# New ranks for the row of maxima and for the two parts of queries and keys in a planned attention stack

## The chip, the cores and the metric

The kernel runs on one core of a Trainium2 chip. The metric is the device time of one execution in microseconds, as a median over runs. A profiled execution gives the trace from which all other times here are read.

## The reference

The input is 16 sequences `x` of 256 tokens with 256 features, and 16 contexts of 120 tokens with 256 features. Four blocks follow each other; all attention has 16 heads of 16 features:

- `l0` and `l1`: cross attention on the context, then `layernorm(attention(x) @ Wo + bo + x)`.
- the third block: causal self attention on 256 tokens (`ms`), cross attention (`cs`) and a feed-forward of 256 to 1024 to 256 features (`ff`), each on a layer norm of `x` and added to `x`.
- `l3`: cross attention with weights rounded to -1, 0 and 1 times a scale, added to `x`.

```python
q = split_heads(x @ Wq.T + bq); k = split_heads(ctx @ Wk.T + bk); v = split_heads(ctx @ Wv.T + bv)
probs = softmax(einsum("bqhd,bkhd->bhqk", q, k) / 4 (+ mask))
x = einsum("bhqk,bkhd->bqhd", probs, v).reshape(B, S, D) @ Wo.T + bo (+ x, layer norm)
```

## The kernel before

Sequences are worked on in pairs: 8 pairs by 6 layers. The pairs of the layers are interleaved by the offsets `OFF`, so that at any time two or three layers are in work.

**Parts.** To keep float32 accuracy from the fast matmul format, a number is held as a high part, rounded to that format, and a low part, the remainder. `split2` makes both for queries and keys out of the projection in PSUM: the high part on ACT (line L784) or on DVE (L785), then the low part on DVE (L787), into a tile `h_q_…` or `h_k_…`. There are three such tiles for all layers. From them SP issues DMAs that stack the parts of each head in rows of `qst` (three issues for a query tile, L826 twice and L829) and `kst` (six issues for keys, L848).

**Maxima.** A first pass of scores (L918 in cross attention, L971 in self attention) goes to PSUM, two banks at a time. DVE reduces them to negated maxima in a tile `neg` (L903, 352 instructions). `put_max` then transposes `neg` on PE (L890, 80 times), copies 32 rows of it out of PSUM as `negt` on ACT or DVE (L423 or L424), and SP writes it as two rows into `qst` (L892). The second pass of scores (L936, L993) multiplies with these rows too, and so has the maximum already subtracted; ACT takes the exponential of it (L907), and PE multiplies with the values (L949, L1009, L1010). The result is transposed on DVE (L855, L871), divided, split and projected (L770); POOL adds it to `x` (L695). L770 is also where the projections of queries, keys and values are.

**The order.** No engine's order is written by hand. `Sched` records every operation with the engines that it may run on, a cost on each, and what it reads and writes. There are 6,364 of them. `run` then plays them through with those costs. An operation joins an engine's queue when the plan has all its inputs ready; when the engine comes free, the one with the lowest key that also finds its buffers goes next. The key is the operation's number in the order of recording, minus what it is put ahead, plus what it is put behind. The order found so is the order of the instructions on each engine; on the chip each engine executes its list in that order and waits on semaphores. SP's DMA issues are ranked in the same way. A running instruction or group of matmuls is not interrupted.

The ranks that stand beside the changed ones: the second pass of scores is 200 ahead (`ST_AHEAD`), the reductions 100 behind (`MAX_BEHIND`), the output projection and the matmuls with the values of a cross attention 200 behind, the mask rows on SP 200 ahead, loads of `x` on SP 50 ahead, the steps of layer norm 50 ahead. `put_max` and `split2` have no rank of their own.

```python
o.key = o.idx - self.ahead                # in op()
heapq.heappush(queue[e], (o.key, o.idx, o))   # in assign()
o.key += MAX_BEHIND                       # in max_op()
```

Of the kernel before, what the change touches and what calls it, by code (L numbers as in the profile page):

```python
# [11 lines left out]
F32 = mybir.dt.float32  # L12
# [8 lines left out]
P = 128  # L21
# [35 lines left out]
X_AHEAD = 50  # L57
SPLIT_AHEAD = 100
SELF_BEHIND = 200
MAGIC = 1.5 * 2.0**23  # L60


# [13 lines left out]
MAX_ROW = MASK_ROW + 1  # L76
# [48 lines left out]
class Sched:  # L125
# [64 lines left out]
    def op(self, alts, r=(), w=(), acq=(), nbytes=0, port=False):  # L190

        o = Op()
        o.alts, o.nbytes, o.port, o.idx = alts, nbytes, port, len(self.ops)
        o.key = o.idx - self.ahead
        deps, uses = set(), []
        for k in (*r, *w, *acq):
            h = k[0] if isinstance(k, tuple) else k
            if h not in uses:
                uses.append(h)
        for k in r:  # L200
            h, sub = k if isinstance(k, tuple) else (k, None)
            hit = False
            for s2, (wr, rd) in h.keys.items():
                if sub is None or s2 is None or s2 == sub:
                    deps.update(wr)
                    rd.append(o)
                    hit = True
            if not hit:
                h.keys[sub] = ([], [o])
        for k in w:  # L210
            h, sub = k if isinstance(k, tuple) else (k, None)
            for s2, (wr, rd) in h.keys.items():
                if sub is None or s2 is None or s2 == sub:
                    deps.update(wr)
                    deps.update(rd)
            if sub is None:
                h.keys.clear()
            h.keys[sub] = ([o], [])
        deps.discard(o)
        o.deps, o.uses = deps, uses  # L220
        for h in uses:
            h.uses += 1
        self.ops.append(o)
        return o
# [119 lines left out]
def cross_stack_kernel(ctx: ExitStack, tc, x, xT, ctxT, mask, w, w1, w2, cols, b1, rows, out):  # L344
    nc = tc.nc
    NP = xT.shape[0] // 2
    ACT, DVE, POOL, PE, SP = nc.scalar, nc.vector, nc.gpsimd, nc.tensor, nc.sync
# [5 lines left out]
    sc = Sched()  # L353
# [14 lines left out]
    def sb(tag, shape, dt, nm, kind=None):  # L368
        return sc.handle(tag, lambda i: work.tile(shape, dt, tag=f"{tag}{i}", name=nm, bufs=1), kind)
# [3 lines left out]
    def bank(nm, kind=None):  # L373
        return sc.handle("ps", lambda i: banks[:, i, :], kind)
# [11 lines left out]
    def pe(cost, fn, r=(), w=(), acq=(), cls="r", ahead=0):  # L386

        o = op({"PE": (cost, fn)}, r, w, acq)
        o.cls = cls
        o.key -= ahead  # L390
        return o
# [8 lines left out]
    def dve(n, fn, r=(), w=(), acq=(), port=False):  # L400
        return op({"DVE": (T_DVE(n), fn)}, r, w, acq, port=port)
# [4 lines left out]
    def dma(fn, nbytes, r=(), w=(), n=1, acq=(), each=420.0, ahead=0):  # L406

        o = op({"SP": (each * n, fn)}, r, w, acq, nbytes)
        o.count = n
        o.key -= ahead  # L410
        return o
# [8 lines left out]
    def cast(n, out, a, r, w, psum_src=False, acq=()):  # L420

        return op({
            "ACT": (T_ACT(n) + (0 if psum_src else 34), lambda: ACT.copy(out(), a())),  # L423
            "DVE": (T_DVE(n if psum_src else n / 2), lambda: DVE.tensor_copy(out(), a())),  # L424
        }, r, w, acq, port=not psum_src)
# [12 lines left out]
    ident = const.tile([P, P], F32, tag="ident", name="ident")  # L438
# [25 lines left out]
    flat = lambda t: t.rearrange("p a b -> p (a b)")  # L464
# [129 lines left out]
    def quant(t, nm):  # L594
# [10 lines left out]
        dve(256, lambda: DVE.tensor_scalar(t(), t(), 2.0, -2.0, ALU.min, ALU.max), r=[t], w=[t], port=True)  # L605
        dve(256, lambda: DVE.tensor_scalar(t(), t(), MAGIC, MAGIC, ALU.add, ALU.subtract), r=[t], w=[t], port=True)
        dve(256, lambda: DVE.tensor_scalar(t(), t(), 1.0, -1.0, ALU.min, ALU.max), r=[t], w=[t], port=True)
# [172 lines left out]

    def split2(ps, src, bias, hi, lo, h2, key, n, r):

        op({
            "ACT": (T_ACT(n, 1), lambda: ACT.activation(hi(), src(), AF.Identity, bias=bias())),  # L784
            "DVE": (T_DVE(n), lambda: DVE.tensor_scalar(hi(), src(), bias(), None, ALU.add)),  # L785
        }, [ps, *r], [(h2, (key, 0))])
        dve(n + 62, lambda: DVE.scalar_tensor_tensor(lo(), src(), bias(), hi().bitcast(F32), ALU.add, ALU.subtract), r=[ps, *r, (h2, (key, 0))], w=[(h2, (key, 1))])  # L787

    def project_heads(W, x_of, bias, high, n, nm, r):

        h2 = sb("h2", [P, 2, 2, S], F32R, f"h2_{nm}")
        ps = bank(f"pj_{nm}")
        br, bcol = ([bias], lambda f: bias()[:, f : f + 1]) if isinstance(bias, Handle) else ([cols_in], lambda f: bias[:, f : f + 1])

        def half_(f):
            o = ps if later.keys else later
            pe(2 * len(terms(W)) * f1(n), lambda: mm_wx(ps()[:, f * S : f * S + n], W, lambda m: m[:, f * P : (f + 1) * P], x_of),
               r=[*W, *r], w=[(ps, f)] if later.keys else [(ps, f), later], acq=[h2])

        def parts(f):  # L800
            split2(ps, lambda: ps()[:, f * S : f * S + n], lambda: bcol(f), lambda: h2()[:, f, high, :n], lambda: h2()[:, f, 1 - high, :n], h2, f, n, br)

        half_(0)
        half_(1)
        parts(0)
        parts(1)

        return h2
# [78 lines left out]
    def put_max(neg, q, nm):  # L887
        ps = bank(f"negp_{nm}")
        negt = sb("negt", [32, P], F32R, f"negt_{nm}")
        pe(110, lambda: PE.transpose(ps()[:, :P], neg(), ident), r=[neg], w=[ps], acq=[negt])  # L890
        cast(128, negt, lambda: ps()[:32, :P], [ps], [negt], psum_src=True)
        dma(lambda: SP.dma_start(flat(q().bitcast(F32))[MAX_ROW : MAX_ROW + 2], negt().bitcast(F32)), 16384, r=[negt], w=[(q, "max")], each=720.0)  # L892

    def new_max():
        neg, made = new_neg()
# [13 lines left out]
    def attend_cross(q, k, b, v, wo, p, nm, x_, dst):  # L909
# [13 lines left out]
        for t in range(2):  # L923
            for j0 in (0, 4):
                s1(t, j0)
        put_max(neg, q, nm)
        t1 = [sb("t1", [P, 2, 8, 32], F32, f"t1_{nm}_{c}") for c in range(2)]

# [28 lines left out]
    def attend_self(q, k, v, wo, p, b, nm, x_):  # L957
# [18 lines left out]
        for t in range(2):  # L976
            for j0 in range(0, 8, 4 >> t):
                s1(t, j0)
        put_max(neg, q, nm)
        t1 = [sb("t1", [P, 2, 8, 32], F32, f"t1_{nm}_{c}") for c in range(2)]  # L980

# [21 lines left out]
        def values(pv, c, pr0, pr1):  # L1003
# [7 lines left out]

            pe(1370, mm, r=[*pr0, pr1, *v], w=[pv], cls="p", ahead=-SELF_BEHIND)

# [326 lines left out]
```

## Time and profile before

| what | value |
|---|---|
| median of 3 runs | 1227.35 us (1226.05 to 1229.39) |
| profiled execution: its own time, its span | 1234.49 us, 1232.8 us |
| busy share of PE, weight loads, DVE, ACT, POOL | 95%, 85%, 78%, 65%, 60% |
| granted TensorE clock, mean | 0.979 of full speed |

PE is TensorE's matmuls and PEld its weight loads, which overlap them; DVE is VectorE, ACT ScalarE, POOL GpSimd, and SP the engine that issues DMAs. A name followed by q (SPq) is the engine's sequencer. In a list of waits a line gives the engine and the work that waited, what it waited for, the sum in us, the number of waits and the longest. In a timeline a line gives start, duration, engine, line, operation, output and inputs, and how many instructions stand in it. The chain of waits is followed back from the last instruction of the execution to what released each one.

### The profile page before, as it was taken

The numbers are of one execution on the slowest core, as the hardware profiler recorded it, in microseconds if no ns is written. First come the engines' busy times: TensorE is split into PE (matmuls) and PEld (weight loads), VectorE is DVE, ScalarE is ACT, GpSimd is POOL, SyncE is SP. The second block draws the span as 40 slices with busy tenths as digits, with TensorE's granted clock in tenths as the row PEclk, the third lists the DMA queues.
The fourth block names the chain that finished last, engine by engine and source line by source line (L and its number), as shares of the span: only waits on it lengthen the run. The fifth ranks groups of instructions, "written<-read, shape, count | busy, mean of one in ns | idle before, by whom it ended". The sixth has DMA issues, their size and how long they took to land.

```text
span 1232.8 us, 29450 instructions
## 1 busy us (share of the span) xinstructions
PE 1169.1 (95%) x10972; PEld 1052.3 (85%) x10972; DVE 958.9 (78%) x1809; ACT 798.1 (65%) x1356; POOL 743.7 (60%) x1011
## 2 busy tenths in 40 slices
PE   6898999999998899999999999998999999999996
PEld 5887788888887788898988888887999999999864
DVE  7687678988886887787798899999634666767886
ACT  4566676667676575677665566677576667766754
POOL 3268566666777797889865556566533236445432
PEclk9799999999998999999999999998999999999989
DMA  8698688666754835544455766772321344435651
GB/s 219 170 257 220 172 243 212 184 179 180 187 142 114 210 101 139 141 131 117 129 148 143 201 169 178 189 197 80 128 76 60 96 112 118 136 91 162 146 129 45
DMA packets 155095, 186.42 MB, mean 151 GB/s; under 512 B 13806, under 2 KB 119624, under 8 KB 154952
## 3 DMA queue, kind: packets, MB, share of 16 engines
q1 hardware_dynamic: 154952, 184.54, 55.7%
q8 instruction: 87, 1.43, 0.5%
q14 instruction: 56, 0.46, 0.1%
HBM read 54.22 MB, written 29.39 MB: 68 GB/s over the span
## 4 chain that ended last, share of the span: by engine, by line
PE 63%; DVE 10%; DMA 8%; POOL 7%; ACT 7%; issue 5%; SPq 1%; POOLq 0%; ACTq 0%; DVEq 0%
PE banks L770 25%; PE banks L918 7%; PE banks L1123 6%; PE banks L936 6%; PE banks L949 6%; DVE neg L903 3%; PE banks L993 3%; PE banks L971 3%; PE banks L737 2%; DMA qst<-h_q_l 2%; PE banks L1009 2%; ACT pr_l L907 1%; POOL pr_ms L1000 1%; DMA qst<-negt_l 1%; DVE t_l L855 1%
## 5 line engine op out<-in xcount | busy, mean ns | idle before, releaser
L903 DVE TENSOR_REDUCE neg<-banks 128x8 f32<-128x960 f32 (+1 forms) x352 | 400.5, 1162 | 53.5 <-PE banks L918 29.8
L907 ACT ACTIVATE pr_l<-banks 120x1024 f32<-120x1024 f32 x192 | 190.0, 1028 | 39.5 <-PE banks L936 37.5
L918 PE MATMUL banks<-kst,qst 97*128 97x240 f32 x1024 | 160.5, 290 | 9.0 <-DMA qst<-h_q_l 2.9
L936 PE MATMUL banks<-qst,kst 99*120 99x256 f32 x1024 | 158.8, 290 | 10.3 <-DMA qst<-negt_l 4.1
L918 PEld LDWEIGHTS banks<-kst,qst 97*128 97x128 f32 x1024 | 136.9, 197 | 24.0 <-issue 10.8
L936 PEld LDWEIGHTS banks<-qst,kst 99*120 99x120 f32 x1024 | 134.9, 186 | 21.7 <-DVE neg L903 7.3
L423 ACT COPY oc<-banks 128x512 f32<-128x512 f32 x94 | 55.1, 587 | 86.0 <-PE banks L770 67.3
L907 ACT ACTIVATE pr_ms<-banks 128x1024 f32<-128x1024 f32 x96 | 95.3, 1032 | 18.4 <-PE banks L993 17.9
L1123 PE MATMUL banks<-w,h1hl_ff 128*128 128x256 f32 x768 | 104.0, 284 | 1.4 <-DVE h1hl_ff L1117 1.3
L770 PE MATMUL banks<-thl_ff,w 128*128 128x256 f32 x768 | 102.2, 283 | 0.1
L695 POOL TENSOR_TENSOR x_l<-oc,x_l 128x512 f32<-128x512 f32 x48 | 62.2, 1295 | 63.6 <-ACT oc L423 63.6
L1123 PEld LDWEIGHTS banks<-w,h1hl_ff 128*128 128x128 f32 x768 | 96.2, 189 | 3.4 <-DVE h1hl_ff L1117 2.3
L949 PE MATMUL banks<-pr_l,vau 120*32 120x256 f32 x1536 | 96.4, 392 | 0.9 <-DVE negt_l L424 0.4
L770 PEld LDWEIGHTS banks<-thl_ff,w 128*128 128x128 f32 x768 | 95.4, 189 | 0.7 <-issue 0.4
L1117 DVE TENSOR_TENSOR h1hl_ff<-h_ff,h1hl_ff 128x512 fp32r<-128x512 f32 x64 | 48.2, 754 | 59.5 <-ACT h1hl_ff L423 56.5
L417 POOL TENSOR_TENSOR cc_l<-t_l,rec_l 128x256 f32<-128x256 f32 x87 | 55.5, 657 | 50.5 <-DVE rec_l L865 48.1
L1000 POOL TENSOR_SCALAR_AFFINE_SELECT pr_ms<-pr_ms 128x512 f32<-128x512 f32 (+1 forms) x96 | 75.4, 800 | 11.3 <-ACT pr_ms L907 11.0
L417 POOL TENSOR_TENSOR cthl_l<-ct_l,cthl_l 128x512 fp32r<-128x512 f32 x42 | 54.1, 1288 | 43.8 <-ACT cthl_l L423 40.1
L1113 ACT ACTIVATE h_ff<-banks,b1t 128x256 f32<-128x256 f32 x119 | 50.3, 472 | 46.5 <-PE banks L770 40.8
L949 PEld LDWEIGHTS banks<-pr_l,vau 120*32 120x32 f32 x1536 | 45.8, 112 | 34.4 <-issue 4.1
L907 ACT ACTIVATE pr_cs<-banks 120x1024 f32<-120x1024 f32 x64 | 64.2, 1029 | 14.6 <-PE banks L936 12.9
L993 PE MATMUL banks<-qst,kst 99*128 99x128 f32 (+1 forms) x512 | 71.2, 281 | 2.6 <-DMA qst<-negt_ms 1.6
(311 smaller groups left out, 2776.5 us busy)
## 6 DMA issues: line engine op xcount, KB each, us to landing
qst<-h_q_l SPq DMA_DIRECT2D x144, 256.0 KB
kst<-h_k_l SPq DMA_DIRECT2D x144, 120.0 KB
kst<-h_k_ms SPq DMA_DIRECT2D x96, 128.0 KB
qst<-h_q_ms SPq DMA_DIRECT2D x48, 256.0 KB
qst<-h_q_cs SPq DMA_DIRECT2D x48, 256.0 KB
xd<-x_l SPq DMA_DIRECT2D x32, 256.0 KB
x_l<-xd SPq DMA_DIRECT2D x32, 256.0 KB
chl_l<-chl SPq DMA_DIRECT2D x16, 512.0 KB
```

What stands on the lines that cost most here:

```text
L417: "POOL": (T_POOL(n, per), lambda: POOL.tensor_tensor(out(), a(), b(), alu)),
L423: "ACT": (T_ACT(n) + (0 if psum_src else 34), lambda: ACT.copy(out(), a())),
L695: pool(512, lambda: POOL.tensor_tensor(fl(), o(), fl(), ALU.add), r=[o, t], w=[t])
L770: PE.matmul(ps, lhs(i, c), rhs(j, c), start=(n == 0), stop=(n == 2 * len(pairs) - 1))
L903: o = dve(2 * n * keys, lambda: DVE.tensor_reduce(out(), src(), AX.X, ALU.max, negate=True), r=[ps, *made], w=[(neg, (t, j0))])
L907: act(1024, lambda: ACT.activation(pr()[:keys], st()[:keys], AF.Exp, scale=0.25), r=[st], w=[pr])
L918: PE.matmul(ps()[:, j // 2, (j % 2) * 2 * SK : (j % 2 + 1) * 2 * SK], q()[:MAX_ROW, j0 + j, t * P : (t + 1) * P], kk(j0 + j)[:MAX_ROW], st ...
L936: PE.matmul(st()[:SK, i, g * S : (g + 1) * S], kk(2 * u + i)[:ROWS, g], q()[:ROWS, 2 * u + i, :], start=True, stop=True)
L949: PE.matmul(pvs[c]()[32 * a : 32 * a + 32, h * S : (h + 1) * S], window(v[0](), c * 8 + a * 2 + h)[:SK], prs[2 * c + h]()[:SK, a // 2, (a ...
L993: PE.matmul(st()[:, i, o * n : (o + 1) * n], k()[:ROWS, j, g, kt * P : (kt + 1) * P], q()[:ROWS, j, kt * P :], start=True, stop=True)
L1000: pool(2 * per * P, lambda: POOL.affine_select(v_(), v_(), pattern=[[0, 2 * per], [1, P]], base=0, channel_multiplier=-1, compare_op=ALU.i ...
L1123: PE.matmul(yo[b]()[:, t * D : (t + 1) * D], hl()[:, i, c * S + t * P : c * S + (t + 1) * P], two(w2s[k // 2][j]())[:, c, :], start=(k == ...
```

## The change

Two operations of `put_max`, the transpose on PE and the DMA on SP, get a key that is 150 lower; the copy between them keeps its key. Both operations of `split2`, the high and the low part of queries and keys, get a key that is 75 higher. No operation is added or removed, and none changes its size.

```diff
+PUT_AHEAD = 150
+
+SPLIT_BEHIND = 75
@@ split2
+        sc.ahead = -SPLIT_BEHIND
         op({
             "ACT": (T_ACT(n, 1), lambda: ACT.activation(hi(), src(), AF.Identity, bias=bias())),
             "DVE": (T_DVE(n), lambda: DVE.tensor_scalar(hi(), src(), bias(), None, ALU.add)),
         }, [ps, *r], [(h2, (key, 0))])
         dve(n + 62, lambda: DVE.scalar_tensor_tensor(lo(), src(), bias(), hi().bitcast(F32), ALU.add, ALU.subtract), r=[ps, *r, (h2, (key, 0))], w=[(h2, (key, 1))])
+        sc.ahead = 0
@@ put_max
-        pe(110, lambda: PE.transpose(ps()[:, :P], neg(), ident), r=[neg], w=[ps], acq=[negt])
+        pe(110, lambda: PE.transpose(ps()[:, :P], neg(), ident), r=[neg], w=[ps], acq=[negt], ahead=PUT_AHEAD)
         cast(128, negt, lambda: ps()[:32, :P], [ps], [negt], psum_src=True)
-        dma(lambda: SP.dma_start(...), 16384, r=[negt], w=[(q, "max")], each=720.0)
+        dma(lambda: SP.dma_start(...), 16384, r=[negt], w=[(q, "max")], each=720.0, ahead=PUT_AHEAD)
```

More of the change, by code (lines that the diff above doesn't have):

```diff
@@ L889, in put_max @@
         negt = sb("negt", [32, P], F32R, f"negt_{nm}")
-        pe(110, lambda: PE.transpose(ps()[:, :P], neg(), ident), r=[neg], w=[ps], acq=[negt])
+        pe(110, lambda: PE.transpose(ps()[:, :P], neg(), ident), r=[neg], w=[ps], acq=[negt], ahead=PUT_AHEAD)
         cast(128, negt, lambda: ps()[:32, :P], [ps], [negt], psum_src=True)
-        dma(lambda: SP.dma_start(flat(q().bitcast(F32))[MAX_ROW : MAX_ROW + 2], negt().bitcast(F32)), 16384, r=[negt], w=[(q, "max")], each=720.0)
+        dma(lambda: SP.dma_start(flat(q().bitcast(F32))[MAX_ROW : MAX_ROW + 2], negt().bitcast(F32)), 16384, r=[negt], w=[(q, "max")], each=720.0, ahead=PUT_AHEAD)
     def new_max():
```

## The prediction

> **What bounds the kernel now.** I began with the page's busy times, then read busy time in stages, then what PE waited for, then the chain of waits, and last two short timelines around a row of maxima.
>
> ```profile
> PE 1169.1 (95%) x10972; PEld 1052.3 (85%) x10972; DVE 958.9 (78%) x1809; ACT 798.1 (65%) x1356; POOL 743.7 (60%) x1011
> ```
>
> ```profile
> 30.00:200.00 170.00, 157.78 (x1447) 138.96 (x1450) 130.06 (x224) 104.59 (x172) 98.02 (x102) 0.95 0.79 210
> 1000.00:1233.00 233.00, 218.22 (x1994) 195.02 (x1992) 171.91 (x328) 153.36 (x275) 106.11 (x144) 0.97 0.45 120
> ```
>
> The last table's columns are the window, its length, busy time of PE, PEld, DVE, ACT and POOL, the granted clock, the DMA share and GB/s. PE is the bound nearly everywhere: 1232.8 - 1169.1 = 63.7 us without a matmul in flight, of which some 11 us fall into the first 30 us. The other gaps are spread: 12.2 us in the first window shown, where DMA is at 0.79, 14.8 us in the second, the rest between. No work is taken away by the change, so all it can win is a part of these gaps. What ended them (engine, work that waited, releaser: sum in us, times, longest):
>
> ```profile
> PE banks L890 <- DVE neg L903: 4.2, 6, 1.9
> PE banks L936 <- DMA qst<-negt_l: 4.1, 3, 2.7
> PE banks L918 <- DMA qst<-h_q_l: 2.9, 3, 1.8
> PE banks L918 <- DVE neg L903: 2.9, 6, 1.2
> ...
> PEld banks L936 <- DVE neg L903: 7.3, 8, 2.9
> PEld banks L918 <- DVE neg L903: 5.7, 11, 1.4
> ```
>
> The reductions (L903) are the most frequent partner: they hold PSUM banks in pairs and they feed the transpose. On PE they end 4.2 + 2.9 us here and 2.0 us in three smaller rows (L936 0.8, L971 0.7, L993 0.5), together 9.1 us; on the weight loads 7.3 + 5.7 us here, and 4.0, 1.7 and 1.1 us for L890, L971 and L993, 19.8 us. The maxima's DMA ends 4.1, 1.6 (negt_ms) and 1.5 us (negt_cs) on PE: 7.2 us. What the splits end themselves on PE (L787 behind L770, L936, L949, L737) is 0.8 + 0.6 + 0.5 + 0.4 + 0.3 = 2.6 us, and the stacks made of them 2.9 us (above) and 0.4 us (kst, before L971), 3.3 us. The chain says the same with other weights:
>
> ```profile
> PE 63%; DVE 10%; DMA 8%; POOL 7%; ACT 7%; issue 5%; SPq 1%; POOLq 0%; ACTq 0%; DVEq 0%
> PE banks L770 25%; PE banks L918 7%; PE banks L1123 6%; PE banks L936 6%; PE banks L949 6%; DVE neg L903 3%; PE banks L993 3%; PE banks L971 3%; PE banks L737 2%; DMA qst<-h_q_l 2%; PE banks L1009 2%; ACT pr_l L907 1%; POOL pr_ms L1000 1%; DMA qst<-negt_l 1%; DVE t_l L855 1%
> ```
>
> L903 has 3% of it, the stack of queries 2%, the row of maxima 1% in the `l` layers. Neither side of the trade is off the path.
>
> **How far a rank reaches.** 6,364 recorded operations over 1232.8 us are 5.2 ranks a microsecond; 150 ranks are 29 us of recording, 75 ranks 14.5 us. A rank decides only between operations that are ready together on one engine; it makes none ready.
>
> **The transpose on PE (80 of about 0.3 us).** Two timelines show what it waits for:
>
> ```profile
> 596.39 2.34 DVE L903 TENSOR_REDUCE neg<-banks 128x4 f32<-128x1024 f32 x2
> 598.27 1.65 PE L770 MATMUL banks<-ms_o,cthl_ms 128*128 128x256 f32 x12
> 599.25 2.58 SPq L848 DMA_DIRECT2D kst<-h_k_ms  x4
> 599.75 0.27 PE L890 MATMUL banks<-ident,neg 128*128 128x128 f32 x1
> 600.48 0.25 ACT L423 CAST negt_ms<-banks 32x128 fp32r<-32x128 f32 x1
> 601.88 0.66 SPq L892 DMA_DIRECT2D qst<-negt_ms  x1
> ...
> 622.75 1.84 PE L1234 MATMUL banks<-cols,w 128*128 128x1 f32 x16
> 624.46 0.31 PE L890 MATMUL banks<-ident,neg 128*128 128x128 f32 x1
> 625.08 0.70 SPq L892 DMA_DIRECT2D qst<-negt_ms  x1
> ```
>
> The last maximum ends at 596.39 + 2.34 = 598.73 and the transpose starts 1.02 us later, right behind a group of 12 matmuls that was already running; at 624.46 it again follows the group that ran when the maximum ended. The next matmuls, the query projection, come after it. A lower key cannot interrupt a group, and here no second group went ahead. I book 0, between a gain of the 4.2 us that PE waits ahead of L890 and, as a transpose chosen before other work can at most displace a group, a loss of its own 80 x 0.3 = 24 us if every one opened a gap (nothing shows one). What hides an earlier transpose is the projection that otherwise runs first; if none is ready, PE has nothing to lose.
>
> **The row on SP (80 issues of 0.69 us).** In the first timeline the copy ends at 600.73 and the issue starts at 601.88, 1.15 us late, because SP was issuing a key stack of four; in the second it is issued at once (624.80 + 0.26 = 625.06, then 625.08). A lower key can remove this lateness, not the flight that follows:
>
> ```profile
> 372.77 5.23 DMA qst<-negt_l
> 676.54 2.37 DMA qst<-negt_ms
> ```
>
> PE's 7.2 us of waits for rows are the most that can go. Seven waits, about half of them behind a late issue, and under 1 us regained in each of those (a half of the 1.15 us): 3.5 x 0.55 = 1.9, booked as -1.5, between 0 and -7.2 us. In return each row that overtakes sets a stack issue back by 0.69 us, and when its copy is late on the chip SP stands still with the stacks behind it; SP already stands 27.0 us for copies by ACT alone in the list of its waits. PE waits for stacks only 3.3 us, so I book +0.5, between 0 and +3.
>
> The Trainium skill's page "DMA: Bandwidth & Descriptors", section "Anatomy of one DMA", puts about 2.0 us of a DMA down to fixed cost, mostly the receipt of the write. By that figure (fitted on GpSimd's path, while SP issues here) most of the 2.37 us flight above would be out of a rank's reach, which speaks against this part; counted strictly, its -1.5 would be 0 and the sum below -3.5.
>
> **The splits behind (512 operations).** The low parts are 256 on DVE at about 0.47 us; of the high parts 185 are on ACT at 0.47 us and 71 on DVE at 0.48 us. No busy time changes. Until now a split went ahead of a reduction recorded up to 100 ranks before it (the reductions are 100 behind); now the lead is 25 ranks. So DVE will more often take a reduction of 1.16 us first, and a layer-norm step, the split following it by one such piece. Gain: a reduction one split (0.47 us) earlier frees two banks and brings the transpose nearer. The waits on L903 bracket it with 9.1 us by PE and 19.8 us by the weight loads; a load that waits delays PE only when nothing is in flight, so I take their middle, 14.5 us, and as a split of 0.47 us earlier is about 40% of a reduction's 1.16 us, I take 40%: -6. Ends: 0 and -13 (two thirds of 19.8).
>
> The page "Perfetto Trace Analysis", section "Identifying the Most-Contended Engine", holds matmul busy time for a bad measure of the room left and takes the share of weight loads. By it the 85% row, not the 95% row, is the one to read, and the term would be 40% of 19.8, that is -8 and a sum of -7; a mean of the two rows stays my value.
>
> Loss: behind a delayed split stand the SP issues of its stack (three for queries, six for keys) and whatever SP has behind them, one of the three h2 tiles, and the bank of the projection. The PE waits on splits and stacks are 2.6 + 3.3 = 5.9 us now. A third more is +2: most stacks land well ahead of the first pass of scores, which the other interleaved layer covers. If that cover is gone, each of these gets longer by a whole reduction. Ends: 0 and +10, see the second rival.
>
> **Sum.** 0 - 1.5 + 0.5 - 6 + 2 = -5 us. The profiled execution took 1234.49 us (span 1232.8 and 1.7 around it), which gives 1229.5 for it. It lies 7.1 us above the median of the runs, 1227.35, and above all three; a shift of the schedule moves both alike, so I predict 1222.4. About 0.3% (3.7 us) is what a measurement can tell from no change, so below 1223.7 counts as faster and above 1231.0 as slower. What is late next is the exponential on ACT (L907 waiting on L936, 37.5 us) and the DMA flights.
>
> **Rival 1: the ranks hardly do anything.** Ready operations rarely compete: ACT and DVE are idle 35% and 22% of the time, the two transposes waited for running groups only, and half of the rows were issued at once. Then the order changes in places, with small gains and losses: 1224 to 1231, say 1227. For it speaks the spread of small waits, against it that one exchange shifts the lists of all five engines after it. Chance 0.24.
>
> **Rival 2: the query stacks become the wait.** Place: the first 400 us, where DMA is at 0.79 and the chain goes through these transfers:
>
> ```profile
> 137.19 5.87 DMA qst<-h_q_l
> 157.22 3.59 DMA qst<-h_q_l
> 162.30 4.04 DMA qst<-h_q_l
> ```
>
> The chain gives them about 2%, some 21 us or five flights of 4 us. If each starts one reduction later, 5 x 1.16 = +5.8 us. A gap then also costs clock: after one in 404.00:408.00 (PE busy 0.59 of 4.00 us) the next 4 us were granted 0.57, or 1.7 us lost. With one such gap more, +7.5 us: 1235. It decides if at least half of the five flights follow a split that DVE now takes after a reduction and the gain on the reductions stays at 0. Against it: the projections of the next pairs cover them now. Chance 0.32.
>
> **How the numbers follow.** The forecast has 0.44, its own range 1213 to 1223.7 (the low end is the sum with -13 and -1.5 and the losses at 0). The whole range reaches to rival 2's price and a little over: 1213 to 1236. Chances: 0.44 faster, 0.24 same, 0.32 slower.
>
> **What would show it.** Right: waits of PE and PEld on DVE L903 fall from 9.1 and 19.8 us by a third; SP issues L892 within 0.1 us of its copy nearly always; busy times stay as they are; gaps fall from 63.7 to about 59 us. Wrong: the chain's DMA qst<-h_q_l above 2%, more waits of L918 and L971 on stacks, more slices with a lowered clock before 400 us. The forecast falls if the waits on L903 shrink and PE's gaps don't, since then another releaser took their place.

## Result and profile after

The changed kernel takes 1241.0 us (median of 4 runs, 1235.5 to 1246.4) where the kernel before, run beside it on the same chip, takes 1228.4 us. The ratio is 1.0084, 95% interval 1.0058 to 1.0111: slower by 12.6 us by the medians. The quotient of the two medians is 1.0103, a little more than the ratio on record; per cents of the change below are the ratio's. The profiled execution after took 1240.46 us with a span of 1238.7; that is only 6.0 us above the profiled execution before, which lay 6 us above its kernel's median. So the two profiles show about half of the loss, and small differences between them are read with care.

The page of the changed kernel, busy times, and then its chain of waits (shares by engine, then by line). Lines of `kernel.py` have moved: L770, L890, L892, L903, L918, L936 and L949 are now L774, L896, L898, L909, L924, L942 and L955.

```profile
PE 1166.6 (94%) x10972; PEld 1052.7 (85%) x10972; DVE 968.2 (78%) x1825; ACT 791.4 (64%) x1339; POOL 748.5 (60%) x1012
```

```profile
PE 59%; DVE 13%; POOL 8%; DMA 6%; ACT 6%; issue 6%; SPq 1%; POOLq 0%; DVEq 0%; ACTq 0%
PE banks L774 24%; PE banks L1129 7%; PE banks L924 7%; PE banks L942 6%; PE banks L955 6%; DVE neg L909 5%; PE banks L999 2%; PE banks L977 2%; PE banks L741 2%; ACT pr_l L913 2%; PE banks L1015 1%; DVE t_l L861 1%; DMA qst<-negt_l 1%; POOL pr_ms L1006 1%; DMA kst<-h_k_ms 1%
```

PE has 1238.7 - 1166.6 = 72.1 us without a matmul (63.7 before). The chain gives the reductions 5% instead of 3%, DVE 13% instead of 10%, and the stack of queries has gone from the list. What ended PE's gaps and the weight loads' (sum in us, times, longest):

```profile
PE banks L774 <- DVE cthl_l L428: 3.6, 2, 3.0
PE banks L924 <- DMA qst<-h_q_l: 3.4, 3, 1.6
PE banks L896 <- DVE neg L909: 3.3, 4, 1.3
PE banks L955 <- DVE neg L909: 3.2, 1, 3.2
PE banks L774 <- POOL cthl_l L421: 2.6, 4, 0.9
PE banks L924 <- DVE neg L909: 2.5, 6, 0.9
...
PE banks L977 <- DVE neg L909: 2.3, 4, 0.9
PE banks L942 <- DMA qst<-negt_l: 2.1, 4, 1.0
...
PEld banks L924 <- DVE neg L909: 7.7, 16, 1.2
```

Adding up all rows of a kind: reductions 9.1 us before, 13.0 after; the turned outputs of attention (`cthl`, high and low part, ahead of the output projection) 6.8 and 10.4; the rows of maxima 7.2 and 2.9; query stacks 2.9 and 3.4, key stacks 0.4 and 1.1. On the weight loads the reductions went from 20.2 us (the prediction's 19.8 leaves out two rows of 0.2) to 24.2 us.

One place shows what a new order can do. Two windows of the kernel before and after, with the prediction's columns (window, length, PE, PEld, DVE, ACT, POOL, granted clock, DMA share, GB/s); first before:

```profile
84.00:88.00 4.00, 4.00 (x36) 3.92 (x35) 2.09 (x6) 3.70 (x7) 2.54 (x2) 1.00 1.10 286
88.00:92.00 4.00, 4.00 (x51) 3.29 (x53) 3.57 (x4) 2.59 (x5) 3.21 (x3) 1.00 1.05 351
```

then after:

```profile
84.00:88.00 4.00, 1.21 (x6) 0.72 (x5) 1.44 (x3) 1.95 (x5) 2.14 (x3) 0.81 1.07 349
88.00:92.00 4.00, 4.00 (x20) 4.00 (x21) 0.00 (x0) 1.26 (x2) 1.69 (x2) 0.50 0.73 244
```

and the timeline of the changed kernel that leads to them (start, duration, engine, line, operation, idle before and its releaser):

```profile
70.13 1.94 ACT L913 ACTIVATE pr_l<-banks 120x1024 f32<-120x1024 f32 x2 [2.37 <-PE banks L942]
...
76.98 1.59 PE L774 MATMUL banks<-l_o,cthl_l 128*128 128x256 f32 x12
...
79.18 2.21 DVE L909 TENSOR_REDUCE neg<-banks 128x8 f32<-128x960 f32 x2
...
79.39 1.93 PE L955 MATMUL banks<-pr_l,vau 120*32 120x256 f32 x32
...
81.31 0.48 DVE L792 SCALAR_TENSOR_TENSOR h_q_l<-banks,cols,h_q_l 128x256 fp32r<-128x256 f32 x1
...
81.70 1.31 DVE L861 STREAM_TRANSPOSE t_l<-banks 128x512 f32<-128x512 f32 x2
...
86.37 0.53 PE L774 MATMUL banks<-l_o,cthl_l 128*128 128x256 f32 x1 [1.97 <-ACT cthl_l L427]
...
87.72 2.71 PE L774 MATMUL banks<-l_o,cthl_l 128*128 128x256 f32 x11 [0.81 <-POOL cthl_l L421]
```

The same attention in the kernel before:

```profile
76.19 1.03 ACT L907 ACTIVATE pr_l<-banks 120x1024 f32<-120x1024 f32 x1
...
76.79 1.93 PE L949 MATMUL banks<-pr_l,vau 120*32 120x256 f32 x32
...
79.37 1.30 DVE L855 STREAM_TRANSPOSE t_l<-banks 128x512 f32<-128x512 f32 x2
...
80.88 2.16 DVE L903 TENSOR_REDUCE neg<-banks 128x8 f32<-128x960 f32 x2
```

After, DVE takes two reductions and then a low part, and turns the output of this attention at 81.70; before, the same turn started at 79.37, ahead of the reductions at 80.88. That looks like DVE's doing, but the turn's input came late. Its matmuls with the values ended on PE at 78.72 before and at 81.32 after, and the turn followed them by 0.65 us before and by 0.38 us after. Nor did these matmuls lack their input: the last exponential that they need had ended at 72.07 after, against 77.22 before. PE's own new list put other groups ahead of them until 79.39, among them the output projection at 76.98. Everything behind the turn (reciprocal, division on POOL, second turn, high and low part) is a chain, and at 84.40 the next entry of PE's list is the projection of this output: PE stands 1.97 and 0.81 us. The plan has the same hole: in its play-through PE is without work for some 3 us ahead of this projection. Then the next 4 us were granted half the clock, and 11 matmuls took 2.71 us where 12 of the same kind took 1.59 at 76.98.

At the same share of all matmuls done, the changed kernel is 4.3 us behind the one before at 109 us, about 1 us behind at 354, about 1 us ahead at 600, and 5 to 6 us behind from 935 us on. So what this place cost was regained; no single place holds the loss, and the place shows how an exchange costs, not where the loss of the whole kernel arises.

The Trainium skill, page "TensorE: Matmul & The Clock Gate", Part 1, "What's actually happening", has the clock go back to half after an idle window of about 3.4 us. In narrower windows of this trace the granted clock was 1.00 up to 86.25 us, 0.50 from 86.50 to 93.25, and 1.00 again from 93.50. So it fell at the end of the first gap of 1.97 us, ahead of the second of 0.81: a single gap as long as the page's window was not needed here.

### The profile page after: what moved, and what is told of

Read it like the earlier page. It is cut to its first block, busy times and chain, and to the rows that moved or that the text cites. A ratio compares the mean times of both kernels' runs of the same rounds, so it can differ in the third digit from the quotient of the medians.

```text
span 1238.7 us, 29440 instructions
## 1 busy us (share of the span) xinstructions
PE 1166.6 (94%) x10972; PEld 1052.7 (85%) x10972; DVE 968.2 (78%) x1825; ACT 791.4 (64%) x1339; POOL 748.5 (60%) x1012
## 4 chain that ended last, share of the span: by engine, by line
PE 59%; DVE 13%; POOL 8%; DMA 6%; ACT 6%; issue 6%; SPq 1%; POOLq 0%; DVEq 0%; ACTq 0%
PE banks L774 24%; PE banks L1129 7%; PE banks L924 7%; PE banks L942 6%; PE banks L955 6%; DVE neg L909 5%; PE banks L999 2%; PE banks L977 2%; PE banks L741 2%; ACT pr_l L913 2%; PE banks L1015 1%; DVE t_l L861 1%; DMA qst<-negt_l 1%; POOL pr_ms L1006 1%; DMA kst<-h_k_ms 1%
## 5 line engine op out<-in xcount | busy, mean ns | idle before, releaser
L909 DVE TENSOR_REDUCE neg<-banks 128x8 f32<-128x960 f32 (+1 forms) x352 | 400.1, 1162 | 58.5 <-PE banks L924 35.1
L924 PE MATMUL banks<-kst,qst 97*128 97x240 f32 x1024 | 160.0, 289 | 11.3 <-DMA qst<-h_q_l 3.4
L942 PE MATMUL banks<-qst,kst 99*120 99x256 f32 x1024 | 156.3, 289 | 7.5 <-DMA qst<-negt_l 2.1
L924 PEld LDWEIGHTS banks<-kst,qst 97*128 97x128 f32 x1024 | 136.1, 196 | 26.0 <-issue 8.4
L942 PEld LDWEIGHTS banks<-qst,kst 99*120 99x120 f32 x1024 | 134.2, 186 | 15.0 <-DVE neg L909 3.3
L774 PE MATMUL banks<-thl_ff,w 128*128 128x256 f32 x768 | 102.7, 284 | 0.0
L955 PE MATMUL banks<-pr_l,vau 120*32 120x256 f32 x1536 | 93.8, 383 | 4.3 <-DVE neg L909 3.2
L774 PEld LDWEIGHTS banks<-thl_ff,w 128*128 128x128 f32 x768 | 95.5, 190 | 1.8 <-issue 1.2
L1123 DVE TENSOR_TENSOR h1hl_ff<-h_ff,h1hl_ff 128x512 fp32r<-128x512 f32 x64 | 50.9, 796 | 47.2 <-ACT h1hl_ff L427 42.9
L955 PEld LDWEIGHTS banks<-pr_l,vau 120*32 120x32 f32 x1536 | 44.7, 109 | 36.8 <-DVE neg L909 3.6
```

Of the source, the lines that this page charges most:

```text
L774: PE.matmul(ps, lhs(i, c), rhs(j, c), start=(n == 0), stop=(n == 2 * len(pairs) - 1))
L909: o = dve(2 * n * keys, lambda: DVE.tensor_reduce(out(), src(), AX.X, ALU.max, negate=True), r=[ps, *made], w=[(neg, (t, j0))])
L924: PE.matmul(ps()[:, j // 2, (j % 2) * 2 * SK : (j % 2 + 1) * 2 * SK], q()[:MAX_ROW, j0 + j, t * P : (t + 1) * P], kk(j0 + j)[:MAX_ROW], st ...
L942: PE.matmul(st()[:SK, i, g * S : (g + 1) * S], kk(2 * u + i)[:ROWS, g], q()[:ROWS, 2 * u + i, :], start=True, stop=True)
L955: PE.matmul(pvs[c]()[32 * a : 32 * a + 32, h * S : (h + 1) * S], window(v[0](), c * 8 + a * 2 + h)[:SK], prs[2 * c + h]()[:SK, a // 2, (a ...
```

## Experiments

Every version is the kernel before with the ranks named; the ratio is against the kernel before on the same chip. The kernel's planner ends its own play-through with a time, got by running `Sched.run` on the recorded operations: 1208.4 us for the kernel before, 1210.4 us for the changed one. It is arithmetic with the kernel's own costs and no time of the chip, but it is known before a run, and the expectations give it. "Shift" is that time against 1208.4. "Clock lost" is the profiled span times (1 - mean granted clock). "Gaps" is the span minus PE's busy time.

| version | shift | ratio [95%] | median us | span, gaps, clock lost |
|---|---|---|---|---|
| before | 0 | 1 | 1228.4 to 1231.3 | 1232.8, 63.7, 25.9 |
| the change | +0.17% | 1.0084 [1.0058, 1.0111] | 1241.0 | 1238.7, 72.1, 26.0 |
| e1_put_only | -0.27% | 0.9930 [0.9912, 0.9948] | 1221.4 | 1220.2, 64.0, 18.3 |
| e1_split_only | +0.94% | 1.0191 [1.0176, 1.0205] | 1253.7 | 1253.7, 76.4, 30.1 |
| e1_hi_only | -0.27% | 0.9986 [0.9972, 1.0000] | 1229.1 | 1229.1, 60.9, 25.8 |
| e1_lo_only | +0.26% | 1.0067 [1.0054, 1.0080] | 1238.7 | 1241.9, 69.9, 34.8 |
| e2_ln49 | +2.40% | 1.0200 [1.0152, 1.0248] | 1255.7 | 1249.8, 81.5, 27.5 |
| e2_put300 | +1.13% | 1.0159 [1.0114, 1.0205] | 1251.8 | 1250.0, 73.8, 32.5 |
| e2_split_ahead75 | +0.24% | 1.0062 [1.0037, 1.0087] | 1239.9 | 1235.2, 68.8, 24.7 |
| e2_split150 | +0.58% | 1.0136 [1.0089, 1.0184] | 1246.5 | 1245.9, 75.8, 29.9 |
| e3_place150 | -0.50% | 0.9966 [0.9946, 0.9985] | 1226.5 | 1221.2, 61.0, 19.5 |
| e3_place150_change | -0.13% | 1.0096 [1.0067, 1.0125] | 1242.8 | 1240.5, 73.3, 29.8 |
| e3_ln49_change | +0.17% | 1.0096 [1.0063, 1.0129] | 1244.7 | 1245.3, 73.2, 33.6 |
| e3_put_max99 | +0.98% | 1.0121 [1.0092, 1.0151] | 1246.4 | 1246.8, 76.5, 31.2 |
| e4_q_only | -0.16% | 1.0010 [0.9992, 1.0028] | 1231.9 | 1232.5, 67.6, 28.3 |
| e4_k_only | +0.44% | 1.0116 [1.0089, 1.0142] | 1245.5 | 1247.2, 67.7, 34.9 |
| e4_stack75 | +0.42% | 1.0147 [1.0125, 1.0169] | 1249.4 | 1247.5, 72.6, 31.2 |
| e5_stack_k75 | 0.0% | 1.0056 [1.0036, 1.0077] | 1237.3 | 1235.1, 70.5, 24.7 |
| e5_stack_q75 | -0.05% | 1.0041 [1.0021, 1.0061] | 1235.6 | 1233.1, 66.1, 23.4 |

**1. Each half by itself.** The question was which half loses, and whether the two add up.

```diff
 e1_put_only:    PUT_AHEAD = 150   SPLIT_BEHIND = 0
 e1_split_only:  PUT_AHEAD = 0     SPLIT_BEHIND = 75
 e1_hi_only:     as split_only, but sc.ahead is back at 0 before the low part
 e1_lo_only:     as split_only, but sc.ahead is set only before the low part
```

> Only the row of maxima is put 150 ahead, on PE and on SP; the splits keep their old ranks. Theory A: 0.995 to 1.001, a small gain or nothing. Theory B: 1.005 to 1.010. Theory C: anywhere within 1%, not fitting a product with the splits alone. The end of the kernel's own plan is 0.3% earlier than before (1205.1).

> Only the splits are put 75 behind; the row of maxima keeps its old ranks. Theory A (delayed splits are what costs): at least the whole loss of the full change, ratio 1.006 to 1.013. Theory B (the earlier row costs, by its overtaking of stacks on SP): 0.998 to 1.002. Theory C (any new rank reorders nearly every list, and the time lands anywhere within about 1% on either side, the parts not adding up): no figure, but the product of this ratio and that of the row alone misses the full change's 1.008 by over 0.005. The end of the kernel's own plan, by its costs, is 0.9% later than before (1219.7 against 1208.4).

> Of the splits only the high parts (185 on ACT, 71 on DVE before) are put 75 behind; low parts and the row keep their ranks. Theory A: a part of the loss, 1.002 to 1.008, as a late high part makes the low part late too. Theory B: 1.000. Theory C: anywhere within 1%. The end of the kernel's own plan is 0.3% earlier than before (1205.1).

> Of the splits only the 256 low parts on DVE are put 75 behind. Theory A: the larger part of the loss, 1.004 to 1.010, since these compete with the reductions on DVE. Theory B: 1.000. Theory C: anywhere within 1%. The end of the kernel's own plan is 0.3% later than before (1211.5).

The rows ahead win 0.7%, the splits behind lose 1.9%. Their product, 1.012, misses the whole change's 1.0084 by 0.004, less than the 0.005 that was asked for as a sign of parts that do not add. The high and low parts show it more clearly: alone they give 1.005 together, where both at once lose 1.019. The rows' gain is not the predicted one either. The busy times of `e1_put_only`:

```profile
PE 1156.2 (95%) x10972; PEld 1042.9 (85%) x10972; DVE 943.6 (77%) x1782; ACT 804.3 (66%) x1383; POOL 744.5 (61%) x1011
```

Its gaps are 64.0 us, those of before 63.7. All 12.6 us of its shorter span are in PE's busy time, with the same 10972 matmuls; 7.6 us of them are clock (25.9 us lost before, 18.3 here), the rest was not taken apart. The profiled execution before lay 6 us above its median, so a part of this difference is between executions and not between kernels: by the medians it is 8.1 us.

**2. Is it the step, or any new order?** A control moves layer norm by one rank, which has nothing to do with the change; others take larger or opposite ranks.

```diff
 e2_ln49:           LN_AHEAD = 49 instead of 50, nothing else
 e2_put300:         PUT_AHEAD = 300   SPLIT_BEHIND = 0
 e2_split_ahead75:  PUT_AHEAD = 0     SPLIT_BEHIND = -75
 e2_split150:       PUT_AHEAD = 0     SPLIT_BEHIND = 150
```

> A control: the kernel before with the layer norm's rank at 49 instead of 50, nothing of the change in it. No mechanism of splits or rows is touched, and one rank is 0.2 us of recording. Theory A (late splits cost through what waits for them): 0.997 to 1.003. Theory C (the time belongs to the particular order that falls out, and any rank moves it): off from 1 by over 0.005. The end of the kernel's own plan is 2.4% later than before (1237.4 against 1208.4); if plan and chip go together, 1.015 to 1.035.

> Only the row of maxima is put ahead, by 300 instead of 150 (150 gave 0.993). Theory R (rows that go earlier win by themselves): 0.988 to 0.996, as far or further. Theory C: anywhere. The end of the kernel's own plan is 1.1% later than before (1222.1); if plan and chip go together, 1.008 to 1.020.

> Only the splits are moved, and the other way: 75 ahead. Theory A (a later split costs because banks and stacks wait for it): an earlier one gains, 0.985 to 0.998. Theory C: anywhere. The end of the kernel's own plan is 0.2% later than before (1211.3); if plan and chip go together, 1.000 to 1.006.

> Only the splits are put behind, by 150 instead of 75 (75 gave 1.019). Theory A: as bad or worse, 1.019 to 1.035. Theory C: anywhere, and less than 1.019 is as likely as more. The end of the kernel's own plan is 0.6% later than before (1215.4; with 75 it was 0.9%); if plan and chip go together, 1.006 to 1.014.

One rank of layer norm costs 2.0%, more than the whole change. It is nearly one place, by the windows of that kernel and one line of its waits:

```profile
936.00:940.00 4.00, 1.45 (x10) 1.24 (x10) 0.00 (x1) 1.21 (x3) 2.53 (x2) 1.00 0.17 66
940.00:944.00 4.00, 0.00 (x0) 0.00 (x0) 0.00 (x0) 1.26 (x3) 2.52 (x2) 0.65 0.66 205
944.00:948.00 4.00, 0.59 (x2) 0.50 (x2) 2.33 (x8) 1.67 (x4) 2.61 (x5) 0.50 0.68 218
948.00:952.00 4.00, 2.64 (x11) 2.38 (x12) 3.97 (x15) 2.34 (x5) 3.21 (x3) 0.50 0.54 169
```

```profile
PE banks L600 <- ACT qa_l_q L599: 9.1, 1, 9.1
```

PE stands 9.1 us for the preparation of the last layer's weights and then works at half clock: that version is 1 us ahead of before at 600 us, about 1 us behind at 894, and 18 us behind at 976. With twice the rank, the rows' gain of 0.7% becomes a loss of 1.6%. The splits lose in both directions (75 ahead 0.6%, 75 behind 1.9%, 150 behind 1.4%), so there is no slope in either knob to believe in.

**3. The same diff on neighbours of the kernel.** If the change has a value of its own, it keeps it when an unrelated constant is moved. `PLACE` is the plan's delay in ns before a freed buffer is taken again.

```diff
 e3_place150:         PLACE = 150.0 instead of 160.0, nothing else
 e3_place150_change:  the change, with PLACE = 150.0
 e3_ln49_change:      the change, with LN_AHEAD = 49
 e3_put_max99:        PUT_AHEAD = 150, SPLIT_BEHIND = 0, MAX_BEHIND = 99 instead of 100
```

> The kernel before with another constant of the plan: a place counts as free 150 ns after its last use instead of 160. Nothing of the change is in it, and no wait on the chip is set by it. If the plan's end ranks versions on the chip (theory P), this one wins, as its plan ends 0.5% earlier than before (1202.3 against 1208.4): 0.985 to 0.997. If only the chip's own accidents decide (theory N), 0.995 to 1.015, as most neighbours so far.

> The full change on top of the 150 ns. The plan ends at 1206.8, 0.1% earlier than before and 0.4% later than the run without the change. Theory P: 0.994 to 1.004, and slower than that run by 0.003 to 0.010. Theory A (late splits cost on the chip whatever the plan): 1.005 to 1.015.

> The full change with the layer norm's rank at 49, which without the change took 1.020. The plan ends at 1210.4, as with the full change alone, and orders PE, ACT and SP as it does. Theory P: 1.004 to 1.012, so that on this neighbour the same diff wins 0.8 to 1.6%. Theory A: 1.025 or more, the loss of the change on top of 1.020.

> Only the row put ahead by 150 (0.993 by itself), with the reductions 99 behind instead of 100. Theory R (the earlier row wins by itself): 0.990 to 0.998. Theory P: its plan ends 1.0% later than before (1220.2), so 1.008 to 1.022.

It does not. The diff costs 0.84% on the kernel before, 1.3% on the neighbour with `PLACE` 150 (0.9966 to 1.0096), and wins 1.0% on the neighbour with `LN_AHEAD` 49 (1.0200 to 1.0096), which had fallen into the stall above; its plan with the change orders PE, ACT and SP as the changed kernel's does, and so does not meet that stall. Against the plan's own shift the diff does keep a sign: it costs 0.7% more than the plan says on the kernel before, 0.9% more with `PLACE` 150 (where 1.0096 lies above the 1.004 that the plan alone allowed) and 1.2% more with `LN_AHEAD` 49. The rows ahead, a gain of 0.7%, are a loss of 1.2% when the reductions move by one rank. So the rows' 0.7% is a property of one order, not of the step.

**4. What the plan does not see.** Over the 18 changed versions, those of this experiment among them, the ratio follows the plan's shift (correlation 0.82). The seven versions that put neither a low part nor a stack behind (the rows', the controls, the high parts, the splits ahead) lie 0.08% beyond it on average (standard deviation 0.33%). The eleven others lie 0.71% beyond it (0.26%), each of them above; the change and the five of experiments 1 to 3 by 0.79%, the five made afterwards by 0.61%. The record has no such division before the results of experiments 1 to 3, and single versions of the two groups overlap (up to 0.46% in the first, from 0.27% in the second). Two explanations were to hand: the banks of the projections are held longer, or the stacks land later than the plan believes. So the splits were separated by kind, and then the SP issues moved without any split.

```diff
 e4_q_only:     SPLIT_BEHIND = 75 for queries alone, PUT_AHEAD = 0
 e4_k_only:     SPLIT_BEHIND = 75 for keys alone, PUT_AHEAD = 0
 e4_stack75:    no split moved; ahead=-75 on the stack DMAs (L826, L829, L848)
 e5_stack_k75:  no split moved; ahead=-75 on the stack DMAs of keys alone
 e5_stack_q75:  no split moved; ahead=-75 on the stack DMAs of queries alone
```

> Only the splits of queries are 75 behind (160 of the 256 pairs); keys and row keep their ranks. The plan ends 0.2% earlier than before (1206.4), so by the plan alone (theory P) 0.994 to 1.002. Theory Q (the extra loss beyond the plan is the query stack, issued right behind its split): 1.004 to 1.012. Theory D (it is DVE falling behind its plan and the bank held meanwhile, whoever's split it is): 1.002 to 1.008, about in proportion.

> Only the splits of keys are 75 behind (96 of the 256 pairs). The plan ends 0.4% later than before (1213.7), so by the plan alone 1.001 to 1.008. Theory Q: the same, since key stacks wait some 10 us for a free key tile anyway. Theory D: 1.005 to 1.011, as the bank is held and DVE reordered here too.

> The splits keep their old ranks, and the DMAs on SP that stack their results are put 75 behind, so that stacks start later while the bank comes free as before. The plan ends 0.4% later than before (1213.4): by the plan alone 1.001 to 1.008. Theory Q: 1.009 to 1.016. Theory D: as by the plan.

> Only the SP issues of the key stacks (six issues a tile) are put 75 behind; the splits and the query stacks keep their ranks. The plan of this kernel ends at 1208.5 us, 0.0% from that of before (1208.4). Theory K (late key stacks cost what the plan does not see): 1.006 to 1.012, some 1235 to 1242 us. Theory P (time follows the plan's end, the rest is scatter of 0.3%): 0.997 to 1.003.

> Only the SP issues of the query stacks (three issues a tile) are put 75 behind; the splits and the key stacks keep their ranks. The plan ends at 1207.8 us, -0.05% from that of before. Theory K (key stacks carry the cost beyond the plan): 0.997 to 1.003. Theory P (time follows the plan's end): 0.996 to 1.003. Against both stands rival 2 of the prediction (query stacks are the wait): 1.006 or more.

Held banks, as a sum, are not what costs: from the end of a projection to the end of its low part, all 256 together, `e4_q_only` holds them 680 us instead of 597 and loses nothing that can be measured, while `e4_k_only` (607 us) loses 1.2% and `e4_stack75` (558 us) 1.5%. With every split in place, late stacks alone lose 1.1% more than the plan's shift; late key splits, which make the key stacks late, 0.7%. For keys the place is seen in the waits of `e5_stack_k75`:

```profile
PE banks L971 <- DMA kst<-h_k_ms: 6.4, 4, 3.1
```

It was 0.4 us, once, before; 6.0 us more, where the median rose by 7.0. But the last pair does not bear out the theory that keys alone carry it: late query stacks cost 0.41%, beyond the 1.003 expected, and late key stacks 0.56%, just under the 1.006 that was asked of them. Both lose, by about half a per cent each; with a scatter of 0.33% from one order to the next, neither by itself tells a late stack from a new order.

Nor do the waits of PE name the stacks elsewhere. Its direct waits for query and key stacks, 3.3 us together before, are 3.5 us in `e4_stack75` and 3.2 us in `e5_stack_q75`, and in `e4_k_only` PE does not wait for a key stack at all (5.7 us for query stacks). So the experiments show that orders with late parts lose more than the plan says; that they lose it because a stack lands late is seen in `e5_stack_k75` alone.

Why the plan would miss it is argued, not shown: by its constants a query stack lands some 2.6 us after its last issue (256 KB at 220 GB/s, and 1.45 us), and the prediction's flights of such stacks took 3.59 to 5.87 us. A stack with that little slack, put behind, arrives after its matmuls were planned. Plans with longer flights were not tried.

## Why the prediction was wrong

The forecast was -5 us, faster, up to 1236; the change costs 12.6. By its steps:

- **The transpose, 0: right**, and more strictly than argued. With the new rank on the transpose alone, the planned order of all five engines is the same as before, instruction for instruction. That identical list was not run on the chip.
- **The row on SP, -1.5: its premise failed.** PE's waits for rows did fall, from 7.2 to 2.9 us. But 43 of 80 rows were issued within 0.1 us of their copy before and 44 after, not "nearly always", and the lateness of all 80 went from 41.3 to 35.7 us. The rows' half alone gave -8 us with unchanged gaps, and that gain is a draw of the order (experiments 2 and 3). (With this term at 0 the prediction's sum is -3.5 us, not below it.)
- **Stacks overtaken on SP, +0.5:** not measured by itself; PE's waits for stacks went from 3.3 to 4.5 us in the change.
- **The reductions earlier, -6: the step that failed.** The term let each reduction start one split (0.47 us) earlier and PE wait less in proportion. From the end of a first pass to the start of its reduction the 352 took 242 us in all before, 235 after, and 207 in `e1_split_only`, the slowest version with split ranks: 0.02 us earlier each in the change, 0.1 us in that version. PE's waits for them still rose from 9.1 to 13.0 us in the change (7.6 in `e1_split_only`, which lost 1.9% all the same), and in `e1_put_only`, where the 352 took 252 us and so started later, PE waited for them only 3.1 us. So reductions hardly came earlier, and PE's waits do not follow how early they come. The sum shortened an average wait, where a wait belongs to a place in a list: at 84 us PE waited for an output whose own matmuls its new list had put late. What made the waits for reductions longer in the change was not traced further.
- **Splits and stacks later, +2: mis-sized.** The step from high to low part grew from 212 to 302 us over 256 parts, 0.35 us each, less than the reduction's 1.16 that was assumed. The direct waits of PE on splits and stacks grew from 5.9 to 7.7 us, as booked. What was missing is what orders with late parts cost beyond the plan, about 0.7% or 8 to 9 us by experiment 4; the direct waits on stacks do not hold it, and its path stays open.
- **Missing from the sum: the clock.** Every term was a gap. In the profiles of the change itself this made no difference: 26.0 us of clock lost against 25.9, with 8.4 us more of gaps. In other versions it did. In `e4_k_only` (profiled in one of its slower executions, 1248.9 us where the median is 1245.5) the span is 14.4 us longer with 4.0 us more of gaps; 9.0 of the rest are clock (34.9 us lost, 25.9 before), as its busy times show:

```profile
PE 1179.5 (95%) x10972; PEld 1058.5 (85%) x10972; DVE 958.4 (77%) x1801; ACT 799.9 (64%) x1364; POOL 742.4 (60%) x1011
```

**Rival 2** had the sign and a price of +7.5 us. Its place was right by half: the gap with a half clock after it does appear at 84 to 92 us, where the DMA share is 1.07, and in `e1_split_only` and `e1_lo_only` too. (The 0.79 that the prediction gives for the first 400 us is that of 30 to 200 us; from 200 to 400 it was 0.65.) But what PE waits for there is the high and low part of an attention's output, not a query stack, whose chain share fell below 1%, and putting the query splits alone behind costs nothing that can be measured. **Rival 1** spoke of small gains and losses in a list that hardly changes. The objection noted against it, that one exchange shifts the lists of all engines, was the better thought: one rank elsewhere moved 2%.

What stays open: which part of the change's 12.6 us belongs to late parts and which is the draw. The plan's shift (+0.17%) and the extra of late parts (0.71%) add to 0.88% against the measured 0.84%, but the change is one of the eleven that give the 0.71%, and with a scatter of some 0.3% for a single version that is agreement, not proof. Two versions beat both kernels, `e1_put_only` (0.9930) and `e3_place150` (0.9966); neither contains a reason that would hold on the next edit.

## What to carry to other kernels

Where a planner writes the orders of all engines, a new rank is first of all a new draw: before believing in a gain or a loss under some 2%, run a neighbour that changes an irrelevant constant by one, and the same edit on that neighbour. Compare the plan's own end before and after; here the sign was the same in 14 of the 17 versions whose shift is not 0.0%. Where the chip exceeds it, ask what the plan books too short; here that was not found, and transfers are one candidate. A term of the form "this operation starts earlier" counts only if the trace shows that PE was waiting for it then; otherwise name what its engine did at that moment before.

## What the hardware showed unexpectedly

Gaps and clock are two prices. In the changed kernel the clock fell to half after one gap of 1.97 us, in the middle of 2.78 us of gap in two pieces: it was 0.81 in the 4 us from 84 on, 0.50 in the next 4 and 0.84 in the 4 after, some 3.4 us lost (0.4 us of it inside the second gap), so the gaps cost about double. Runs of one kernel share this: the four runs of the changed kernel lie between 1235.5 us at a mean granted clock of 0.984 and 1246.4 us at 0.973, and 0.011 of 1240 us is 13.6 us, more than the whole spread of 10.9. The weight loads' busy share, the other measure weighed in the prediction, stayed at 84 to 86% in versions with spans from 1220 to 1254 us, too coarse to tell most of them apart; the matmuls' share, 93 to 95%, did no better.
